# First block of a time-mix and feed-forward kernel: k's first products token tile by token tile, with part of k's weights loaded ahead of x's third tile

## Chip, cores and metric

One core of one Trainium2 chip runs the whole kernel. The metric is the device time of one execution in microseconds (us), read as the median of several runs. Three runs of the kernel before took 940.05, 940.10 and 938.86 us.

## What is computed

For x of shape (4, 1024, 512), float32, with xn the layer norm of x over its last axis, the kernel computes x + attention(xn) + ffn(xn):

```python
xx = concatenate([xn[:, 1:2], xn[:, :-1]], axis=1) - xn      # the token before, less this one
k = (xn + xx * time_mix_k) @ Wk.T                            # 512 -> 704
r = (xn + xx * time_mix_r) @ Wr.T
state_t = state_{t-1} * exp(-exp(time_decay)) + relu(k_t)    # a scan over the tokens
attention = layernorm((state * r) @ Wv.T) * gamma + beta     # 704 -> 512
ffn = (gelu(f16(xn) @ W0.T + bias0)).f16 @ W1.T + bias1      # 512 -> 2048 -> 512
```

Token 0 of a sequence takes token 1 as "the token before".

## The kernel before, in words

The 4096 tokens are cut into eight blocks of 512 tokens (`TB`), each of four tiles of 128 tokens (`NS`). The 512 channels are four chunks of 128 (`NC`), the 704 hidden rows five chunks of 128 and a half chunk. A block is turned so that channels lie on the partitions; then come the products of k and r (`product`, L213), the scan, the output product (L448, L458), and the feed-forward part (`up` L517, `down` L532). Every block but the first is normed and turned while TensorE works on the block before. The first block has nothing ahead of it, so it has a function of its own, `first_inputs`, and only that stretch and its loads are touched by the change.

Loads. All DMAs are issued on SyncE's queue, in the order of the code: x's four tiles (L83, 256 KB each), the two mixing vectors (L108, L109, 2 KB each, as `mix_rows`), k's four weight tiles (L113, 352 KB each), three small loads into `late_rows` (L114 to L116: decay and bias0), r's weights (L118), then W0 and the rest. The issuing engine waits for the DMA eight places earlier to land.

`first_inputs`. Within `tc.manual_schedule` the order on ScalarE, VectorE and TensorE is the order of the code:

- `busy(10)` (L238): ten products of the identity with itself, whose result nobody reads. `mix_rows` is turned on TensorE (L299), and ScalarE copies it out as `mix_sb` and `rest_sb` = 1 - mix (L309, L310).
- Tiles 0 and 1 of x: mean and variance (L186, L187), root on ScalarE (L244), reciprocal on VectorE (L247), normalised (L190), turned on TensorE into the four PSUM tiles `pt` (L254), and `busy(2)`.
- `mixed(0, c, ...)` for half a block (256 tokens) and each chunk c: ScalarE writes rest * now into `xk` (L267), VectorE adds mix * the token before (L279). The first column takes a product on ScalarE (L274, `other`) and a sum on GpSimd (L277).
- `products(c, half)`: for each chunk c three products (hidden chunks 0 to 2) of 128x128 weights with 256 tokens, into the PSUM tiles `pk_0`, `pk_1`, `pk_2`.
- Tiles 2 and 3 are normed and turned while the first half's products run. Between the third and fourth chunk of those products TensorE also turns `late_rows` (L325) into the PSUM tile `tail`. Then the second half is mixed and multiplied.
- ScalarE copies `tail` out as `late_sb` (L332). Then `mixed(1, c, 0, TB)`: the same for r over all 512 tokens, ScalarE into `ar` (pool tag `xx`, two buffers), VectorE into `xnT` (L267, L279).
- After the schedule: ScalarE casts `pt` to float16 (L341), copies the last column (L343), loads another table and makes exp(-exp(decay)) in place (L345, L346).

What follows on TensorE is `full_chunks`: `pr_0`, `pr_1`, `pr_2` (r's products, four of 512 tokens each, from `xnT`), then `pk_3`, `pr_3`, `pk_4`, `pr_4`. On ScalarE `states` reads `pk_0` as `rk_0` (Relu, L389), then `rk_1`, `rk_2`; VectorE scans them (L391).

PSUM. The pool `ps_mm` has four buffers, handed out in turn: `idle`, `small`, `tail`, `pk_0`, then again `pk_1` (idle's), `pk_2` (small's), `pr_0` (tail's), `pr_1` (pk_0's, free once `rk_0` has read it), `pr_2` (pk_1's, after `rk_1`). This order is the same in both kernels.

Of the kernel before, what the change touches and what calls it, by code (L numbers as in the profile page):

```python
# [9 lines left out]
F32 = mybir.dt.float32  # L10
F32R = mybir.dt.float32r
AF = mybir.ActivationFunctionType
ALU = mybir.AluOpType

P = 128
# [4 lines left out]
def time_mix_and_gelu_ffn(  # L20
# [26 lines left out]
    nc = tc.nc  # L47
    B, T, C = x.shape
    HID = wkT.shape[1]
    N = w0T.shape[1]  # L50
    TB = 512
    NS = TB // P
    NC = C // P
    NN = N // P
# [3 lines left out]
    NF = HID // P  # L58
# [5 lines left out]
    def pool(name, bufs, **kw):  # L64
        return ctx.enter_context(tc.tile_pool(name=name, bufs=bufs, **kw))
# [4 lines left out]
    const = pool("const", 1)  # L70
    one = pool("one", 1)
    two = pool("two", 2)
    three = pool("three", 3)
    four = pool("four", 4)
    ps_mm = pool("ps_mm", 4, space=bass.MemoryType.PSUM)
    ps_e = pool("ps_e", 4, space=bass.MemoryType.PSUM)
    dram = pool("dram", 1, space=bass.MemoryType.DRAM)

    def load_x(i):
        b, t0 = blocks[i]  # L80
        xs = one.tile([P, NS, C], F32, tag="x", name=f"x_{i}")
        for s in range(NS):
            nc.sync.dma_start(xs[:, s, :], x[b, t0 + s * P : t0 + (s + 1) * P, :])  # L83
        return xs


    x_now = load_x(0)
    ident = const.tile([P, P], F32, name="ident")
    make_identity(nc, ident)
    nhalf = const.tile([P, NS], F32, name="nhalf")  # L90
# [3 lines left out]
    eps_sb = const.tile([P, 1], F32, name="eps_sb")  # L94
    nc.vector.memset(eps_sb, EPS)
    mix_rows = const.tile([2 * NC, P], F32, name="mix_rows")
    late_rows = const.tile([NF + 1 + NN, P], F32, name="late_rows")
    nc.vector.memset(late_rows, 0.0)
    mix_sb = const.tile([P, 2 * NC], F32, name="mix_sb")
# [5 lines left out]
    def rows(ap):  # L105
        return ap.rearrange("(c p) -> c p", p=P)

    nc.sync.dma_start(mix_rows[:NC], rows(mix_k))  # L108
    nc.sync.dma_start(mix_rows[NC:], rows(mix_r))  # L109
    wk_sb = [const.tile([P, HID], F32, name=f"wk_{c}") for c in range(NC)]  # L110
    wr_sb = [const.tile([P, HID], F32, name=f"wr_{c}") for c in range(NC)]
    for c in range(NC):
        nc.sync.dma_start(wk_sb[c], wkT[c * P : (c + 1) * P, :])  # L113
    nc.sync.dma_start(late_rows[:NF], rows(decay[:H0]))  # L114
    nc.sync.dma_start(late_rows[NF : NF + 1, :HF], decay[H0:].rearrange("(c p) -> c p", p=HF))
    nc.sync.dma_start(late_rows[NF + 1 :], rows(bias0))  # L116
# [59 lines left out]
    def rstd_of(var, name):  # L176

        n = var.shape[1]
        r = two.tile([P, n], F32, tag=f"rstd{n}", name=name)
        nc.gpsimd.tensor_scalar_add(r, var, EPS)  # L180
        nc.gpsimd.tensor_tensor(r, r, nhalf[:, :n], ALU.pow)
        return r

    def stats_of(mv, s, src, name):
        st6 = two.tile([P, 6], F32, tag="st6", name=name)
        nc.vector.bn_stats(st6, src)  # L186
        nc.vector.bn_aggr(mv[:, s, :], st6)  # L187

    def normalize(dst, src, mean, rstd):
        nc.vector.tensor_scalar(dst, src, mean, rstd, ALU.subtract, ALU.mult)  # L190
# [21 lines left out]
    def product(dst, w, cols, src, c):  # L212
        return nc.tensor.matmul(  # L213
            dst, w[c][:, cols], src, start=(c == 0), stop=(c == NC - 1)
        )

    def first_inputs(xs, behind):

        pts = [ps_e.tile([P, TB], F32, tag="pe", name=f"pt_0_{c}") for c in range(NC)]
        idle = ps_mm.tile([P, TB], F32, tag="mm", name="idle")
        small = ps_mm.tile([P, TB], F32, tag="mm", name="small")
        mix_t = small[:, : 2 * NC]
        tail = ps_mm.tile([P, TB], F32, tag="mm", name="tail")
        late_t = tail[:, : NF + 1 + NN]
        mv = two.tile([P, NS, 2], F32, tag="mv", name="mvx_0")
        rstd = two.tile([P, NS], F32, tag=f"rstd{NS}", name="rx_0")  # L230
        xk = one.tile([P, NC, TB], F32, tag="xk", name="xk_0")
        TH = TB // 2
        halves = slice(0, TH), slice(TH, TB)

        def busy(n):

            for _ in range(n):
                nc.tensor.matmul(idle[:, :P], ident, ident, start=True, stop=True)  # L238

        def stats(s):  # L240
            stats_of(mv, s, xs[:, s, :], f"stx_0_{s}")

        def deviations(a, b):
            nc.scalar.activation(rstd[:, a:b], mv[:, a:b, 1], AF.Sqrt, bias=eps_sb)  # L244

        def inverses(a, b):
            nc.vector.reciprocal(rstd[:, a:b], rstd[:, a:b])  # L247

        def normalized(s):
            normalize(xs[:, s, :], xs[:, s, :], mv[:, s, 0:1], rstd[:, s : s + 1])  # L250

        def turned(s):
            for c in range(NC):
                nc.tensor.transpose(  # L254
                    pts[c][:, s * P : (s + 1) * P], xs[:, s, c * P : (c + 1) * P], ident
                )

        def mixed(kind, c, a, b):

            src = pts[c]  # L260
            if kind == 0:
                dst = part = xk[:, c, :]
            else:
                part = two.tile([P, TB], F32, tag="xx", name=f"ar_0_{c}")
                dst = xnT[:, c, 1:]
            j = kind * NC + c
            scaled = nc.scalar.activation(  # L267
                part[:, a:b], src[:, a:b], AF.Identity, scale=rest_sb[:, j : j + 1]
            )

            if a == 0:

                other = four.tile([P, 1], F32, tag="other", name=f"other_{kind}_{c}")
                nc.scalar.activation(  # L274
                    other, src[:, 1:2], AF.Identity, scale=mix_sb[:, j : j + 1]
                )
                nc.gpsimd.tensor_add(dst[:, 0:1], part[:, 0:1], other)  # L277
                a = 1
            added = nc.vector.scalar_tensor_tensor(  # L279
                dst[:, a:b],  # L280
                src[:, a - 1 : b - 1],
                mix_sb[:, j : j + 1],
                part[:, a:b],
                ALU.mult,
                ALU.add,
            )
            return scaled, added

        def products(c, part):
            for h, pk in enumerate(pks):  # L290
                product(pk[:, part], wk_sb, slice(h * P, (h + 1) * P), xk[:, c, part], c)

        with tc.manual_schedule(
            engines={nc.scalar.engine, nc.vector.engine, nc.tensor.engine}
        ):

            nc.scalar.activation(rstd[:, :1], eps_sb, AF.Sqrt)
            busy(10)
            nc.tensor.transpose(mix_t, mix_rows, ident[: 2 * NC, : 2 * NC])  # L299
            stats(0)  # L300
            deviations(0, 1)
            stats(1)
            deviations(1, 2)
            for s in range(NS // 2):
                inverses(s, s + 1)
                normalized(s)
                turned(s)
            busy(2)
            nc.scalar.copy(mix_sb, mix_t)  # L309
            nc.scalar.activation(rest_sb, mix_t, AF.Identity, bias=1.0, scale=-1.0)  # L310
            pks = [ps_mm.tile([P, TB], F32, tag="mm", name=f"pk_0_{h}") for h in range(3)]
            stats(2)
            for c in range(NC):
                if c == NC - 1:
                    stats(3)
                mixed(0, c, 0, TH)
            deviations(2, NS)
            inverses(2, NS)
            normalized(2)
            normalized(3)  # L320
            for c in range(NC):
                if c == NC - 1:
                    turned(2)
                    turned(3)
                    nc.tensor.transpose(  # L325
                        late_t, late_rows, ident[: NF + 1 + NN, : NF + 1 + NN]
                    )
                products(c, halves[0])
            for c in range(NC):
                mixed(0, c, TH, TB)  # L330
                products(c, halves[1])
            nc.scalar.copy(late_sb, late_t)  # L332
            for c in range(NC):
                scaled, added = mixed(1, c, 0, TB)

        behind.enter_context(tc.issue_after(scaled.ins))
        behind.enter_context(tc.issue_after(added.ins))
        x16s = []
        for c, pt in enumerate(pts):
            x16 = four.tile([P, TB], F16, tag="x16", name=f"x16_0_{c}")  # L340
            nc.scalar.copy(x16, pt)  # L341
            x16s.append(x16)
            nc.scalar.copy(last[:, c, :], pt[:, TB - 1 :])  # L343

        nc.scalar.activation(w_sb, w_sb, AF.Exp)  # L345
        nc.scalar.activation(w_sb, w_sb, AF.Exp, scale=-1.0)  # L346
        return x16s, xk, pks
# [214 lines left out]
    state = {}  # L562
    behind = ExitStack()
    x16s, xk, pks = first_inputs(x_now, behind)
    xf = ffn_input(0, x16s)

# [6 lines left out]
    for i in range(len(blocks)):  # L573
# [6 lines left out]
        if more:  # L580

            with tc.issue_after(state["kept"].ins) if i == 1 else nullcontext():
                x_now = load_x(i + 1)
# [76 lines left out]
```

## Time and profile before

| | |
|---|---|
| median of the three runs | 940.05 us |
| the profiled execution, its own time | 939.56 us |
| its span, first instruction to last | 937.5 us |
| TensorE busy | 930.5 us, 99% |
| ScalarE busy | 164.4 us, 18% |
| VectorE busy | 489.0 us, 52% |
| first product of `pk` starts | 8.66 us |
| first product of `pr` starts | 20.33 us |
| granted TensorE clock | 1.00 throughout |

The span lies within the execution's own time; 2.06 us lie around it. Starts are counted from the span's first instruction. A float32 product of 128x128 weights shows as two records of TensorE (MATMUL) with two weight loads (PEld, which overlap it); a turn shows as one. [...] records overlap: what a stream of them costs is the distance from start to start.

### The profile page before, as it was taken

What the parts mean: (1) busy time and instruction counts of PE and PEld (TensorE: products, weight loads), DVE (VectorE), ACT (ScalarE), POOL (GpSimd) and SP (SyncE); (2) the same over time, 40 slices, a digit from 0 to 9 for tenths busy, and PEclk for the clock granted to TensorE, in tenths of its full rate; (3) what the DMA queues carried; (4) which work ended last, traced back from release to release, by engine and by line L of the source; (5) the groups of instructions that cost most, each with busy time, mean ns of one, the idle gap of its engine ahead of it and who ended that gap; (6) DMA issues with size and microseconds to landing.
All of it is one profiled execution on the core that took longest, in us unless ns stands there. A gap on an engine that the chain in (4) does not pass through costs nothing.

```text
span 937.5 us, 8775 instructions
## 1 busy us (share of the span) xinstructions
PE 930.5 (99%) x3266; PEld 591.2 (63%) x3266; DVE 489.0 (52%) x843; ACT 164.4 (18%) x276; POOL 52.5 (6%) x132
## 2 busy tenths in 40 slices
PE   8999999999999999999999999999999999999998
PEld 7448854885448854588545884458844688445686
DVE  6768772733836338353474525755256552642513
ACT  6423410220002200112001220012100121001021
POOL 1010000000100001000010000100011000100100
PEclk9999999999999999999999999999999999999999
DMA  9644660443204432054320543105431044310243
GB/s 318 202 155 157 224 224 0 135 158 113 90 1 157 143 106 90 1 170 143 104 77 0 180 145 114 56 0 195 142 113 45 19 138 152 96 45 1 69 155 113
DMA packets 39718, 106.50 MB, mean 114 GB/s; under 512 B 4447, under 2 KB 4732, under 8 KB 39676
## 3 DMA queue, kind: packets, MB, share of 16 engines
q1 hardware_dynamic: 39676, 105.94, 34.3%
q8 instruction: 26, 0.43, 0.2%
q14 instruction: 16, 0.13, 0.0%
HBM read 89.14 MB, written 16.78 MB: 113 GB/s over the span
## 4 chain that ended last, share of the span: by engine, by line
PE 99%; DMA 0%; SPq 0%; DVE 0%; issue 0%; ACT 0%; DVEq 0%; POOL 0%; ACTq 0%
PE pd L517 25%; PE pe L532 25%; PE po L448 15%; PE pk L213 15%; PE pr L213 15%; PE pkr L213 3%; PE po L458 2%; DMA mix_rows<-in_L_attn_time_mix_r 0%; SPq L83 0%; PE pt L254 0%; DVE e L495 0%; ACT xk L267 0%; DVE z L504 0%; SPq L108 0%; DVEq L656 0%
## 5 line engine op out<-in xcount | busy, mean ns | idle before, releaser
L532 PE MATMUL pe<-w,d 128*128 128x512 f32 x1024 | 250.4, 389 | 0.0
L532 PEld LDWEIGHTS pe<-w,d 128*128 128x128 f32 x1024 | 192.2, 188 | 40.2 <-DVE d L527 0.3
L517 PE MATMUL pd<-xf,w0h 128*128 128x512 f32 x512 | 202.8, 396 | 0.0
L517 PE MATMUL pd<-xf,w0l 128*128 128x512 f32 x512 | 199.5, 390 | 0.0
L527 DVE CAST d<-d 128x512 fp32r<-128x512 f16 x128 | 54.3, 425 | 187.9 <-ACT d L525 186.6
L525 ACT ACTIVATE d<-pd,late_sb 128x512 f16<-128x512 f32 x128 | 87.9, 687 | 352.9 <-PE pd L517 352.9
L213 PE MATMUL pk<-xk,wk 128*128 128x512 f32 (+1 forms) x344 | 144.0, 563 | 0.6 <-POOL xk L277 0.6
L213 PE MATMUL pr<-xnT,wr 128*128 128x512 f32 x320 | 143.7, 592 | 0.0
L448 PE MATMUL po<-wv_sb,g 128*128 128x512 f32 x320 | 140.8, 595 | 0.0
L213 PEld LDWEIGHTS pk<-xk,wk 128*128 128x128 f32 x344 | 65.2, 190 | 72.2 <-issue 67.9
L517 PEld LDWEIGHTS pd<-xf,w0h 128*128 128x128 f32 x512 | 96.1, 188 | 23.2 <-issue 2.3
L517 PEld LDWEIGHTS pd<-xf,w0l 128*128 128x128 f32 x512 | 96.2, 188 | 21.6 <-issue 1.9
L213 PEld LDWEIGHTS pr<-xnT,wr 128*128 128x128 f32 x320 | 60.6, 189 | 76.4 <-issue 74.9
L448 PEld LDWEIGHTS po<-wv_sb,g 128*128 128x128 f32 x320 | 60.2, 190 | 75.8 <-issue 75.0
L207 DVE STREAM_TRANSPOSE xnT<-x 32x512 f32<-32x512 f32 x112 | 78.7, 702 | 5.0 <-PE pkr L213 2.9
L389 ACT ACTIVATE rk<-pk 128x512 f32<-128x512 f32 x40 | 23.9, 597 | 255.7 <-PE pk L213 253.5
L186 DVE BATCH_NORM_STATS2 sty<-po 128x6 f32<-128x512 f32 x32 | 22.1, 691 | 68.3 <-PE po L458 66.1
L391 DVE TENSOR_TENSOR_SCAN st<-late_sb,carry,rk 128x512 f32<-128x512 f32 (+1 forms) x24 | 30.7, 1279 | 43.9 <-ACT rk L389 43.9
L417 DVE TENSOR_TENSOR g<-st,pr 128x512 f32<-128x512 f32 x40 | 27.4, 684 | 39.1 <-PE pr L213 39.1
L391 DVE TENSOR_TENSOR_SCAN st<-late_sb,rk 128x512 f32<-128x512 f32 (+1 forms) x24 | 29.2, 1218 | 32.7 <-ACT rk L389 31.0
L180 POOL TENSOR_SCALAR ry<-mvy 128x1 f32<-128x1 f32 x32 | 11.4, 357 | 436.6 <-DVE mvy L187 436.6
L495 DVE TENSOR_TENSOR e<-pe,b_sb 128x512 f16<-128x512 f32 x32 | 20.2, 685 | 18.3 <-PE pe L532 18.3
(69 smaller groups left out, 455.6 us busy)
## 6 DMA issues: line engine op xcount, KB each, us to landing
w<-w1d SPq DMA_DIRECT2D x111, 512.0 KB, 3.3
x<-in_L_attn_x SPq DMA_DIRECT2D x32, 256.0 KB, 5.2
xres<-in_L_attn_x SPq DMA_DIRECT2D x32, 256.0 KB, 2.7
w1d<-w SPq DMA_DIRECT2D x16, 512.0 KB, 2.9
out<-z SPq DMA_DIRECT2D x31, 256.0 KB, 2.6
w0raw<-in_L_ffn_W SPq DMA_DIRECT2D x16, 256.0 KB, 3.3
w1raw<-in_L_ffn_W SPq DMA_DIRECT2D x16, 256.0 KB, 3.4
wk<-in_L_attn_Wk SPq DMA_DIRECT2D x4, 352.0 KB, 4.9
```

The source lines that it names most:

```text
L186: nc.vector.bn_stats(st6, src)
L207: nc.vector.transpose(dst[i * Q : (i + 1) * Q, :, :, j, :], src[j * Q : (j + 1) * Q, :, :, i, :],)
L213: return nc.tensor.matmul(dst, w[c][:, cols], src, start=(c == 0), stop=(c == NC - 1))
L389: nc.scalar.activation(rk[:hw], pk, AF.Relu)
L391: nc.vector.tensor_tensor_scan(st[:hw], w_sb[:hw, h : h + 1].to_broadcast([hw, TB]), rk[:hw], 0.0 if t0 == 0 else carry[:hw, h : h + 1], A ...
L417: nc.vector.tensor_mul(g[:, h, :], st, pr)
L448: nc.tensor.matmul(pos[s], g[:, h, s * P : (s + 1) * P], wv_sb[:, h, :], start=(first and h == 0), stop=(not first and h == NF - 1),)
L495: nc.vector.tensor_add(e16, pe, b1_sb)
L517: nc.tensor.matmul(pd, w[c][:, cols], xf[:, c, :], start=(c == 0 and w is w0h), stop=(c == NC - 1 and w is w0l),)
L525: state["gelu"] = nc.scalar.activation(d16, pd, AF.Gelu, bias=b0_sb[:, n : n + 1])
L527: nc.vector.tensor_copy(d, d16)
L532: nc.tensor.matmul(pe[s], d[:, s * P : (s + 1) * P], w1[part], start=(n == 0 and part == 0), stop=(n == NN - 1 and part == 1),)
```

## The change

The two `mix_rows` loads go from SyncE's queue to ScalarE's. k's weights come in two parts: columns 0 to 383 of all four tiles (four DMAs of 192 KB) after x's second tile, the remaining 320 columns (four of 160 KB) after x's fourth. In `first_inputs` each token tile of 128 is normed, turned, mixed and multiplied on its own: `products` takes 128 tokens instead of 256. Tile 0 keeps root and reciprocal; tiles 1 to 3 take theirs from `rstd_of` (two instructions on GpSimd, L180, L181). The first column is made by one ScalarE instruction that reads the column just written as its bias. The ten `busy` products become five, then the turn of `mix_rows`, then five; `busy(2)` becomes `busy(3)` after tile 0. The turn of `late_rows` goes behind all products of `pk`.

```diff
-    def load_x(i):
+    def load_x(i, amid=lambda: None):
         b, t0 = blocks[i]
         xs = one.tile([P, NS, C], F32, tag="x", name=f"x_{i}")
         for s in range(NS):
+            if s == NS // 2:
+                amid()
             nc.sync.dma_start(xs[:, s, :], x[b, t0 + s * P : t0 + (s + 1) * P, :])
...
+    FIRST = 3
+    def load_wk(cols):
+        for c in range(NC):
+            nc.sync.dma_start(wk_sb[c][:, cols], wkT[c * P : (c + 1) * P, cols])
+
+    x_now = load_x(0, lambda: load_wk(slice(0, FIRST * P)))
...
-    nc.sync.dma_start(mix_rows[:NC], rows(mix_k))
-    nc.sync.dma_start(mix_rows[NC:], rows(mix_r))
...
-    for c in range(NC):
-        nc.sync.dma_start(wk_sb[c], wkT[c * P : (c + 1) * P, :])
+    nc.scalar.dma_start(mix_rows[:NC], rows(mix_k))
+    nc.scalar.dma_start(mix_rows[NC:], rows(mix_r))
+    load_wk(slice(FIRST * P, HID))
...
         def stats(s):
             stats_of(mv, s, xs[:, s, :], f"stx_0_{s}")
+            var = mv[:, s, 1:]
+            if s == 0:
+                rstds[s] = dev[:, :1]
+                nc.scalar.activation(rstds[s], var, AF.Sqrt, bias=eps_sb)
+                nc.vector.reciprocal(rstds[s], rstds[s])
+            else:
+                rstds[s] = rstd_of(var, f"rx_0_{s}")
...
             if a == 0:
-                other = four.tile([P, 1], F32, tag="other", name=f"other_{kind}_{c}")
-                nc.scalar.activation(
-                    other, src[:, 1:2], AF.Identity, scale=mix_sb[:, j : j + 1]
-                )
-                nc.gpsimd.tensor_add(dst[:, 0:1], part[:, 0:1], other)
+                scaled = nc.scalar.activation(
+                    dst[:, 0:1], src[:, 1:2], AF.Identity, scale=m, bias=part[:, 0:1]
+                )
                 a = 1
...
-            nc.scalar.activation(rstd[:, :1], eps_sb, AF.Sqrt)
-            busy(10)
+            nc.scalar.activation(dev[:, 1:2], eps_sb, AF.Sqrt)
+            busy(5)
             nc.tensor.transpose(mix_t, mix_rows, ident[: 2 * NC, : 2 * NC])
-            stats(0)
-            deviations(0, 1)
-            stats(1)
-            deviations(1, 2)
-            for s in range(NS // 2):
-                inverses(s, s + 1)
-                normalized(s)
-                turned(s)
-            busy(2)
+            busy(5)
             nc.scalar.copy(mix_sb, mix_t)
             nc.scalar.activation(rest_sb, mix_t, AF.Identity, bias=1.0, scale=-1.0)
-            pks = [ps_mm.tile([P, TB], F32, tag="mm", name=f"pk_0_{h}") for h in range(3)]
-            stats(2)
-            for c in range(NC):
-                if c == NC - 1:
-                    stats(3)
-                mixed(0, c, 0, TH)
-            deviations(2, NS)
-            inverses(2, NS)
-            normalized(2)
-            normalized(3)
-            for c in range(NC):
-                if c == NC - 1:
-                    turned(2)
-                    turned(3)
-                    nc.tensor.transpose(
-                        late_t, late_rows, ident[: NF + 1 + NN, : NF + 1 + NN]
-                    )
-                products(c, halves[0])
-            for c in range(NC):
-                mixed(0, c, TH, TB)
-                products(c, halves[1])
+            stats(0)
+            normalized(0)
+            turned(0)
+            busy(3)
+            stats(1)
+            pks = [
+                ps_mm.tile([P, TB], F32, tag="mm", name=f"pk_0_{h}") for h in range(FIRST)
+            ]
+            for s in range(NS):
+                tokens = slice(s * P, (s + 1) * P)
+                for c in range(NC):
+                    if c == NC // 2 and s + 1 < NS:
+                        normalized(s + 1)
+                    mixed(0, c, tokens.start, tokens.stop)
+                for c in range(NC):
+                    if c == NC - 1 and s + 1 < NS:
+                        turned(s + 1)
+                    products(c, tokens)
+                if s + 2 < NS:
+                    stats(s + 2)
+            nc.tensor.transpose(late_t, late_rows, ident[: NF + 1 + NN, : NF + 1 + NN])
             nc.scalar.copy(late_sb, late_t)
             for c in range(NC):
                 scaled, added = mixed(1, c, 0, TB)
```

More of the change, by code (lines that the diff above doesn't have):

```diff
@@ L82, in load_x @@
         for s in range(NS):
+            if s == NS // 2:
+                amid()
             nc.sync.dma_start(xs[:, s, :], x[b, t0 + s * P : t0 + (s + 1) * P, :])
         return xs
-    x_now = load_x(0)
+    FIRST = 3
+    wk_sb = [const.tile([P, HID], F32, name=f"wk_{c}") for c in range(NC)]
+    wr_sb = [const.tile([P, HID], F32, name=f"wr_{c}") for c in range(NC)]
+    def load_wk(cols):
+        for c in range(NC):
+            nc.sync.dma_start(wk_sb[c][:, cols], wkT[c * P : (c + 1) * P, cols])
+    x_now = load_x(0, lambda: load_wk(slice(0, FIRST * P)))
     ident = const.tile([P, P], F32, name="ident")
@@ L106, in rows @@
         return ap.rearrange("(c p) -> c p", p=P)
-    nc.sync.dma_start(mix_rows[:NC], rows(mix_k))
-    nc.sync.dma_start(mix_rows[NC:], rows(mix_r))
-    wk_sb = [const.tile([P, HID], F32, name=f"wk_{c}") for c in range(NC)]
-    wr_sb = [const.tile([P, HID], F32, name=f"wr_{c}") for c in range(NC)]
-    for c in range(NC):
-        nc.sync.dma_start(wk_sb[c], wkT[c * P : (c + 1) * P, :])
+    nc.scalar.dma_start(mix_rows[:NC], rows(mix_k))
+    nc.scalar.dma_start(mix_rows[NC:], rows(mix_r))
+    load_wk(slice(FIRST * P, HID))
     nc.sync.dma_start(late_rows[:NF], rows(decay[:H0]))
@@ L229, in first_inputs @@
         mv = two.tile([P, NS, 2], F32, tag="mv", name="mvx_0")
-        rstd = two.tile([P, NS], F32, tag=f"rstd{NS}", name="rx_0")
+        dev = two.tile([P, NS], F32, tag=f"rstd{NS}", name="rx_0")
+        rstds = {}
         xk = one.tile([P, NC, TB], F32, tag="xk", name="xk_0")
-        TH = TB // 2
-        halves = slice(0, TH), slice(TH, TB)
         def busy(n):
@@ L241, in stats @@
             stats_of(mv, s, xs[:, s, :], f"stx_0_{s}")
[L243 to L247, printed above, removed]
+            var = mv[:, s, 1:]
[5 more added lines that the diff above has]
+                rstds[s] = rstd_of(var, f"rx_0_{s}")
         def normalized(s):
-            normalize(xs[:, s, :], xs[:, s, :], mv[:, s, 0:1], rstd[:, s : s + 1])
+            normalize(xs[:, s, :], xs[:, s, :], mv[:, s, 0:1], rstds[s])
         def turned(s):
@@ L266, in mixed @@
             j = kind * NC + c
+            m = mix_sb[:, j : j + 1]
             scaled = nc.scalar.activation(
@@ L271, in mixed @@
             if a == 0:
-                other = four.tile([P, 1], F32, tag="other", name=f"other_{kind}_{c}")
-                nc.scalar.activation(
-                    other, src[:, 1:2], AF.Identity, scale=mix_sb[:, j : j + 1]
+                scaled = nc.scalar.activation(
+                    dst[:, 0:1], src[:, 1:2], AF.Identity, scale=m, bias=part[:, 0:1]
                 )
-                nc.gpsimd.tensor_add(dst[:, 0:1], part[:, 0:1], other)
                 a = 1
             added = nc.vector.scalar_tensor_tensor(
[L280 to L285, printed above, removed]
+                dst[:, a:b], src[:, a - 1 : b - 1], m, part[:, a:b], ALU.mult, ALU.add
             )
```

## The prediction

> **What bounds the kernel now.** I read the page first. TensorE is busy for the whole span; no other engine comes near.
>
> ```profile
> PE 930.5 (99%) x3266; PEld 591.2 (63%) x3266; DVE 489.0 (52%) x843; ACT 164.4 (18%) x276; POOL 52.5 (6%) x132
> ```
>
> Then the waits of TensorE over the whole span. There are three, all of them ahead of the first product of `pk` at 8.66 us:
>
> ```profile
> PE idle L238 <- POOL ident masks.py:199: 1.3, 1, 1.3
> PE small L299 <- DMA mix_rows<-in_L_attn_time_mix_r: 0.6, 1, 0.6
> PE pk L213 <- POOL xk L277: 0.6, 1, 0.6
> ```
>
> From 8.66 us on TensorE never waits. So whatever makes a product late from there on is paid in full at the end, and only work taken from it, or an earlier start, is a gain. What TensorE does in the first 31 us, from its timeline (start, length, operation):
>
> ```profile
> 1.34 4.45 PE L238 MATMUL idle<-ident 128*128 128x128 f32 x20 [1.34 <-POOL ident masks.py:199]
> ...
> 7.48 0.61 PE L238 MATMUL idle<-ident 128*128 128x128 f32 x4
> 8.66 4.12 PE L213 MATMUL pk<-xk,wk 128*128 128x256 f32 x18 [0.57 <-POOL xk L277]
> 12.62 1.04 PE L254 MATMUL pt<-ident,x 128*128 128x128 f32 x8
> 13.59 0.24 PE L325 MATMUL tail<-ident,late_rows 22*128 22x22 f32 x1
> 13.75 6.74 PE L213 MATMUL pk<-xk,wk 128*128 128x256 f32 x30
> 20.33 10.47 PE L213 MATMUL pr<-xnT,wr 128*128 128x512 f32 x24
> ```
>
> The reader is to see that `tail` is turned at 13.59, in the middle of `pk`. ScalarE's timeline shows what hangs on that:
>
> ```profile
> 14.81 0.20 ACT L332 COPY late_sb<-tail 128x22 f32<-128x22 f32 x1
> 14.87 0.73 ACT L267 ACTIVATE ar<-pt,rest_sb 128x512 f32<-128x512 f32 x1
> ...
> 18.09 0.59 ACT L341 CAST x<-pt 128x512 f16<-128x512 f32 x1
> ...
> 20.40 1.28 ACT L345 ACT_TABLE_LOAD   x1
> 21.70 0.21 ACT L345 ACTIVATE late_sb<-late_sb 128x6 f32<-128x6 f32 x1
> 21.81 0.58 ACT L389 ACTIVATE rk<-pk 128x512 f32<-128x512 f32 x1
> ```
>
> Behind the copy of `tail` stand r's inputs (`ar`), the casts, the table and `rk_0`, which ends at 22.39. All this runs under the products of `pk` and `pr_0`. `pr_1`, which writes into `pk_0`'s buffer, starts at 20.33 + 8 x 0.43 = 23.77 (8 records of `pr_0`; 24 of them take 10.47 less a last one's tail), so `rk_0` has 1.4 us to spare.
>
> **What the Trainium skill says.** "PSUM — Partial Sum Buffer", Engine vs sequencer instructions: ScalarE's queue is strict FIFO, and TensorE's matmuls run in program order, only weight loads being pulled ahead. The timelines agree: `ar` starts 0.06 us behind the copy of `tail`, never ahead of it. "ScalarE: Activation LUTs", What ACT_TABLE_LOAD costs: 1283 ns for a table, here 1.28 us; each pointer operand (scale or bias from a column) adds about 93 ns. Here a 512-column Gelu with a bias takes 687 ns and the Relu without one 597 ns, so it agrees (90). "TensorE: Matmul & The Clock Gate", The HAM clock gate: the array runs at half rate until busy for about 3.4 us and falls back after an idle window of that length. Here the distance of the idle products goes from 0.21 to 0.11 us about 4 us after the first; no idle time after 8.66 tests the fall.
>
> **The change part by part.**
>
> *Loads.* 1.4 MB of weights and 1 MB of x stay what they are; two issues of 0.38 and 0.26 us leave SyncE's queue, four of 0.43 are added to it, each past `late_rows`, r's weights and W0. That is about 1.1 us later for these at most. r's last tile was issued at 9.3 and lands within 5 us, at 14.3; it is needed from 20 us. W0's splits start at 22.4. Cover enough; I take zero. x's tiles 2 and 3 get 0.8 MB ahead of them, some 2 us at the 400 GB/s of 6 to 10 us: they land by about 8.5 and are wanted at 9.4 and 12. k's first columns have some 1.3 MB before and with them: about 6 us, wanted from 7.4. The mixing vectors, issued at 0.7 on ScalarE ahead of its table load, should land by 3.6 (x's first tile takes 2.7 us); if they take a microsecond more the root of tile 0 waits 0.5 us.
>
> *First product.* Mean and variance of tile 0 still start at 3.40 and end at 4.30. Root 4.41 to 4.70, reciprocal 0.13, normalise 0.55, hand-over 0.04 each: 5.45. TensorE is in `busy` until about 5.7 (5 products at 2 x 0.213 = 2.1 us, the turn of the vectors at 3.5, then 2.1 us that speed up at 5.35). First turn 0.33: 6.03. ScalarE: 0.10 to wake, 128 columns 0.35 (0.47 for 256, 0.73 for 512, so 0.13 per 128), then the column: it reads what was just written, so it waits for the end (0.06), and has two pointers (0.25 for L274, plus 0.09): 6.9. VectorE 0.04 + 0.35; TensorE 0.10: 7.4. That is 1.25 us ahead of 8.66.
>
> *Products.* 24 products of 256 tokens become 48 of 128. The idle products are the same shape: (0.61 - 0.275) / 3 = 0.111 us from record to record, so 48 x 0.222 = 10.66 us, against 24 x 2 x 0.216 = 10.36. Turns: 12 x 0.109 = 1.31 against 8 x 0.109 = 0.87. The turn of `late_rows` (0.15) leaves. After each turn the next tile's first `xk` needs 0.27 (turn), 0.10, 0.35, 0.04, 0.35, 0.10 = 1.21 us, while TensorE has three further turns and three products, 1.1 us: about 0.1 us idle, four times. VectorE's 2.5 us a tile and GpSimd's 0.92 (0.36 + 0.57 in the later rows) fit into TensorE's 3.1. So `pk` ends at 7.4 + 10.66 + 1.31 + 0.45 = 19.8 against 20.33: a gain of 0.5, the start half spent.
>
> *The turn of `late_rows`.* It now ends the stretch, at 19.8 + 0.24 = 20.05. ScalarE has the copy ahead of `ar` in its order, so `ar_0` starts at 20.05 + 0.10 + 0.06 = 20.2 instead of 14.87. The first `xnT`: 0.73 (ScalarE), 0.06 + 0.36 (column), 0.04 + 0.75 (VectorE), 0.10: `pr_0` starts at 22.25 instead of 20.33. This is a wait of 2.1 us on TensorE that did not exist: behind it everything.
>
> *`rk_0`.* In the trace of before, `ar_0` to the first cast takes 3.22 us and the cast to the end of `rk_0` 4.30 (18.09 to 22.39: casts, table, exp). The second is unchanged. The first becomes about 4.15: two times 0.73 + 0.06 + 0.36 - 0.10 overlapped, then two `ar` that wait for VectorE to free a buffer. So `rk_0` ends at 20.2 + 4.15 + 4.30 = 28.65, and `pr_1`, next in TensorE's order with nothing to pass it, starts at 28.75. `pr_0` will have ended at about 26.2, so 2.5 us more stand idle. Against 23.77 that is **+5.0 us**. If the column costs no more than before (0.25), four columns and the tile-0 path give back 0.6, and waits of 0.1 that don't occur 0.4: +4.0 is the lower end.
>
> *Behind.* `rk_1` needs the scan of `rk_0` (1.23) and 0.6: 30.6, while `pr_1` runs to 32.2; `pr_2` does not wait. W0's splits start some 6 us later, TensorE 5. The first of them is needed at 48.14 and was complete at 30.13. The tightest is `g_4`: ready at 50.37 for 51.83, and it loses one microsecond of 1.46 but now stands ahead of a split in VectorE's order. I take zero.
>
> Sum: 939.56 + 5.0 = 944.5 for an execution like the profiled one. That one lies 0.5 below the median, so the forecast is 944.7, between 944.5 and 945.0.
>
> **The rivals.**
>
> *The clock falls back.* Two idle stretches of 2.1 and 2.5 us, with 4 us of products between, are each shorter than the window, but the window runs free. If it falls, `pr_1` runs at half rate for some 3.4 us: +1.7, 946.4. For it: nothing in this trace. Against: the gap of 0.63 at 5.8 did not slow what followed.
>
> *The tile stretch is bound by the small engines.* ScalarE and VectorE hand over per chunk; if each chunk of 0.67 us waited another 0.1, 16 of them cost 1.6: 946.2. Against: both have slack of 0.6 us a tile.
>
> *Only the first wait shows.* If `pr_1` did not have to wait for `rk_0`, the loss is 22.25 - 20.33 = 1.9: 941.7. Against: the buffers go round in turn.
>
> *The gain comes through (not slower).* If the copy of `tail` does not hold `ar`, everything for r runs under `pk` as now, and the earlier end of 0.5 counts: 939.3. It decides at one point: `rk_0` must end by 23.7, so with 8.5 us of work from the copy, that must start by 15.2, and the turn it waits for stands behind 48 products that end near 20. Only if the order were not kept.
>
> **How the numbers follow.** The likeliest case, 943.2 to 945.8, has 0.77; clock or small engines 0.15 together (to 946.8); first wait only 0.04; gain 0.04. The range 943.1 to 946.7 leaves out the last two and some of the tails. The measurement tells about 0.2%, 1.9 us, from no change. Slower by more: 0.92; within: 0.06; faster: 0.02.
>
> **What would show it.** `pk`'s first record near 7.4 and 128-token records 0.111 apart; `pr_0` at 22 us behind a wait that ends in VectorE's `xnT`; `pr_1` at 28 to 29 behind ScalarE's `rk`; two new rows in TensorE's waits, 2.1 and 2.5 us. If the copy of `late_sb` runs before 16 us, or `pr_1` starts before `rk_0` ends, the forecast is wrong.

## Result and profile after

The kernel after takes 944.71 us, median of six runs (944.12 to 944.92); six runs of the kernel before beside it took 939.33 us (938.86 to 940.10). The ratio is 1.0051, 95% interval 1.0040 to 1.0062: slower, by 5.4 us. The profiled execution took 944.66 us with a span of 942.9 us. TensorE is still the busy engine; it has 3.4 us more, though the arithmetic is the same (24 products became 48 of half the length).

```profile
PE 933.9 (99%) x3316; PEld 594.1 (63%) x3316; DVE 489.7 (52%) x849; ACT 166.7 (18%) x282; POOL 54.1 (6%) x130
```

TensorE's waits over the whole span (total, times, longest): two new ones, in front of `pr`. The one for `mix_rows` is gone.

```profile
PE pr L222 <- DVE xnT L286: 2.0, 1, 2.0
PE idle L245 <- POOL ident masks.py:199: 1.3, 1, 1.3
PE pr L222 <- ACT rk L383: 0.9, 1, 0.9
PE pk L222 <- DVE xk L286: 0.3, 1, 0.3
```

TensorE's timeline up to 34 us:

```profile
3.97 2.50 PE L245 MATMUL idle<-ident 128*128 128x128 f32 x10
6.27 0.64 PE L263 MATMUL pt<-ident,x 128*128 128x128 f32 x4
6.75 0.83 PE L245 MATMUL idle<-ident 128*128 128x128 f32 x6
7.88 2.29 PE L222 MATMUL pk<-xk,wk 128*128 128x128 f32 x18 [0.29 <-DVE xk L286]
...
16.90 3.63 PE L222 MATMUL pk<-xk,wk 128*128 128x128 f32 x30
20.45 0.23 PE L325 MATMUL tail<-ident,late_rows 22*128 22x22 f32 x1
22.71 5.40 PE L222 MATMUL pr<-xnT,wr 128*128 128x512 f32 x8 [2.03 <-DVE xnT L286]
29.00 5.42 PE L222 MATMUL pr<-xnT,wr 128*128 128x512 f32 x12 [0.89 <-ACT rk L383]
```

`pk` starts 0.78 us earlier than before and ends at the same time, 20.5. Then come the turn of `late_rows`, 2.03 us of nothing, `pr_0`, and again 0.89 us of nothing: `pr_1` starts at 29.00 instead of 23.77. ScalarE's timeline shows what TensorE waits for:

```profile
20.73 0.18 ACT L326 COPY late_sb<-tail 128x22 f32<-128x22 f32 x1 [2.81 <-PE tail L325]
20.80 0.69 ACT L277 ACTIVATE ar<-pt,rest_sb 128x512 f32<-128x512 f32 x1
21.52 0.35 ACT L282 ACTIVATE xnT<-pt,ar,mix_sb 128x1 f32<-128x1 f32 x1
...
24.66 0.57 ACT L335 CAST x<-pt 128x512 f16<-128x512 f32 x1
...
26.96 1.28 ACT L339 ACT_TABLE_LOAD   x1
28.26 0.21 ACT L339 ACTIVATE late_sb<-late_sb 128x6 f32<-128x6 f32 x1
28.37 0.58 ACT L383 ACTIVATE rk<-pk 128x512 f32<-128x512 f32 x1
```

The reader is to see the bracket of the first line: ScalarE stands idle for 2.81 us until TensorE has turned `tail`, though all it needs for `ar` has long been there. From the copy to the end of `rk_0` it never stops again: 8.2 us in one row.

One thing more is in this trace. The eight records of `pr_0` take 6.29 us from 22.71 to 29.00 less 0.89 of waiting: 5.4 instead of 3.44. The granted clock by stretches (stretch; its length, TensorE's busy time and records; **clock**; the two columns for DMA) says why:

```profile
20.00:23.00 3.00, 0.97 (x7) 1.00 0.99 275
23.00:24.00 1.00, 1.00 (x3) 0.71 0.98 227
24.00:27.00 3.00, 3.00 (x5) 0.53 0.97 341
27.00:29.00 2.00, 1.11 (x3) 1.00 0.99 351
```

TensorE ran at half its clock from 23.42 to 26.83 us. Whether that is part of the price was the first open question.

### The profile page after: what moved, and what is told of

Same layout as the page of the kernel before. It is cut to its first block, busy times and chain, and to the rows that moved or that the text cites. A ratio compares the mean times of both kernels' runs of the same rounds, so it can differ in the third digit from the quotient of the medians.

```text
span 942.9 us, 8892 instructions
## 1 busy us (share of the span) xinstructions
PE 933.9 (99%) x3316; PEld 594.1 (63%) x3316; DVE 489.7 (52%) x849; ACT 166.7 (18%) x282; POOL 54.1 (6%) x130
## 4 chain that ended last, share of the span: by engine, by line
PE 98%; ACT 1%; DVE 0%; issue 0%; POOL 0%; DVEq 0%; POOLq 0%; ACTq 0%
PE pd L511 25%; PE pe L526 25%; PE po L442 15%; PE pk L222 15%; PE pr L222 14%; PE pkr L222 3%; PE po L452 2%; PE idle L245 1%; ACT ar L277 0%; ACT x L335 0%; PE pt L263 0%; ACT xnT L282 0%; ACT L339 0%; DVE e L489 0%; ACT rk L383 0%
## 5 line engine op out<-in xcount | busy, mean ns | idle before, releaser
L222 PE MATMUL pr<-xnT,wr 128*128 128x512 f32 x320 | 145.8, 598 | 2.9 <-DVE xnT L286 2.0
L222 PEld LDWEIGHTS pk<-xk,wk 128*128 128x128 f32 x392 | 67.5, 190 | 71.0 <-issue 68.2
```

The lines of the kernel that those rows point to most:

```text
L222: return nc.tensor.matmul(dst, w[c][:, cols], src, start=(c == 0), stop=(c == NC - 1))
```

## Experiments

The theory: ScalarE executes in order, so the late turn of `late_rows` makes everything behind its copy late, first `ar` and `xnT` (the first wait), then, behind the casts and the table, `rk_0` (the second). Rivals: the cutting into tiles of 128 tokens with its small instructions; the loads; the clock.

All kernels in one table (us). "pk", "pr_0", "pr_1" are the first records in the profiled execution; "rest" is that execution's own time less the start of `pr_1`; the runs of before stand beside the median.

| kernel | pk | pr_0 | pr_1 | profiled | rest | median | before beside | ratio, 95% interval |
|---|---|---|---|---|---|---|---|---|
| before | 8.66 | 20.33 | 23.77 | 939.56 | 915.79 | 939.33 | | |
| after | 7.88 | 22.71 | 29.00 | 944.66 | 915.66 | 944.71 | 939.33 | 1.0051 (1.0040–1.0062) |
| e1 turn early | 7.52 | 20.25 | 25.72 | 943.04 | 917.32 | 942.44 | 939.78 | 1.0029 (1.0017–1.0040) |
| e2 before, turn last | 8.96 | 22.44 | 28.24 | 944.06 | 915.82 | 945.25 | 939.78 | 1.0055 (1.0042–1.0068) |
| e3 before, loads | 10.11 | 23.47 | 26.91 | 942.46 | 915.55 | 940.30 | 939.78 | 1.0008 (1.0000–1.0017) |
| e4 Relu first | 7.64 | 22.47 | 27.71 | 943.30 | 915.59 | 943.26 | 939.78 | 1.0036 (1.0023–1.0049) |
| e5 gap busy | 7.31 | 22.29 | 28.46 | 945.89 | 917.43 | 944.92 | 939.80 | 1.0059 (1.0046–1.0072) |
| e6 Relu first, gap busy | 7.32 | 22.29 | 25.92 | 941.52 | 915.60 | 941.60 | 939.80 | 1.0019 (1.0011–1.0028) |
| e7 turn early, Relu first | 9.00 | 22.41 | 25.85 | 941.38 | 915.53 | 939.70 | 939.80 | 1.0001 (0.9992–1.0009) |
| e8 as e7, fewer idle | 7.40 | 20.06 | 23.50 | 939.14 | 915.64 | 938.91 | 939.80 | 0.9991 (0.9983–0.9999) |
| e9 gap partly busy | 7.99 | 22.87 | 26.57 | 942.12 | 915.55 | 941.65 | 939.89 | 1.0022 (1.0013–1.0030) |
| e10 before, mixing vectors | 8.77 | 20.44 | 23.88 | 939.57 | 915.69 | 939.25 | 939.89 | 0.9989 (0.9981–0.9998) |

Read the column "rest" first. But for e1 and e5 (their clock falls behind `pr_1`) it lies within 0.3 us. So nothing behind `pr_1` tells these kernels apart, and each profiled time follows from the start of its `pr_1`.

**e1: only the turn, forward again.**

```diff
                         turned(s + 1)
+                        if s + 2 == NS:
+                            nc.tensor.transpose(late_t, late_rows, ...)
...
-            nc.tensor.transpose(late_t, late_rows, ...)
```

> The kernel after, with only the turn of late_rows moved forward: behind the turn of tile 3, ahead of the last products of tile 2. The cutting into tiles of 128 tokens and the loads stay. If the place of the turn is the cause, ScalarE copies tail right behind its last xk, at about 17.9 us, so everything on ScalarE comes 2.9 us earlier: ar_0 at 17.9 instead of 20.8, rk_0 ends at 26.1 instead of 29.0. pr_0 then follows pk at about 20.5 without a wait, and the one wait left is that of pr_1 for rk_0, about 2.1 us: pr_1 at 26.1, and the time is 941.8 us. If the cutting into tiles, the small engines or the loads are the cause, the place of the turn changes nothing: 944.7.

`ar_0` starts at 17.48 and `rk_0` ends at 25.67; the first wait is gone and the second is as expected:

```profile
PE pr L222 <- ACT rk L386: 1.9, 1, 1.9
```

The six executions split by their mean clock over the span: with 1.000 they took 940.96, 941.79 and 941.83 us, as the theory has it; with 0.998 they took 943.04, 943.58 and 943.58. The profiled one is of the second kind. Its clock by stretches shows the fall right behind the wait that ends at 25.72:

```profile
24.00:27.00 3.00, 1.28 (x2) 0.85 1.01 309
27.00:29.00 2.00, 2.00 (x4) 0.50 1.04 386
29.00:34.00 5.00, 5.00 (x13) 0.95 0.67 213
```

The place of the turn costs 2.3 us by the medians, 2.9 where the clock holds. The rival that the cutting or the loads cost it all falls. My 941.8 left out that the remaining wait brings a fall of the clock half the time.

The wait that is left comes from the rest of the change, as the traces show; no run takes it alone. `ar` needs all four tiles, and tile 3 is turned at 16.11 here, while before both later tiles are turned from 12.62 on. So `ar_0` starts at 17.48 instead of 14.87 although the turn of `late_rows` holds nothing up. The new first-column instruction makes the way from `ar_0` to the first cast 3.90 us instead of 3.22. Together `rk_0` ends 3.28 us later than before, where it had 1.4 to spare: 1.87 us of waiting.

**e2: only the late turn, in the kernel before.**

```diff
-                    nc.tensor.transpose(late_t, late_rows, ...)
                 products(c, halves[0])
...
+            nc.tensor.transpose(late_t, late_rows, ...)
```

> The kernel before, with only the turn of late_rows moved behind all products of pk; first block, loads and halves as before. If the place of the turn is the cause, the loss appears without anything else of the change: pk ends at 20.3, the turn at 20.5, ar_0 at 20.6, pr_0 at 22.4 behind a wait of 1.9 us (the column here takes one ScalarE and one GpSimd instruction that lie beside the column's long sum), pr_1 at 20.6 + 3.2 + 4.3 = 28.2 instead of 23.8: +4.4, 943.7 us. If the cutting, the small engines or the loads are the cause, it stays at 939.3.

```profile
PE pr L213 <- POOL xnT L277: 1.8, 1, 1.8
...
PE pr L213 <- ACT rk L387: 0.4, 1, 0.4
```

The same two waits, and `pr_1` at 28.24 for 28.2 expected: the move of one turn, alone, brings 4.5 of the 5.2 us in the start of `pr_1`, and a median as high as that of the kernel after (945.25 against 939.78). The late turn and the rest of the change each make `rk_0` late, and the later one counts, so the gains and losses of e1 and e2 do not add. In the profiled execution (944.06) the clock fell in `pr_0` and the fall lies ahead of the second wait. Three of the five executions took 945.25 to 945.78; of these there is no trace, so what the 1.2 to 1.7 us above the profiled one are stays open. All five have a mean clock of 0.998; a fall that comes behind the second wait, as in the trace of e5 below, would fit, but is not shown.

**e3 and e10: only the loads, in the kernel before.** e3 takes both parts (as in the change's own diff), e10 only the mixing vectors:

```diff
-    nc.sync.dma_start(mix_rows[:NC], rows(mix_k))
-    nc.sync.dma_start(mix_rows[NC:], rows(mix_r))
+    nc.scalar.dma_start(mix_rows[:NC], rows(mix_k))
+    nc.scalar.dma_start(mix_rows[NC:], rows(mix_r))
```

> The kernel before, with only the change's loads: the mixing vectors on ScalarE's queue, k's weights in two parts around x's third and fourth tile. The prediction took them at nothing: the first product of pk stays at 8.7, pr_1 at 23.8, the time at 939.3 within 0.4. The wait for mix_rows of 0.6 us may go, but the first product waits for xk, not for it. If x's third and fourth tile come too late behind the weights, the second half's products wait, and the time is over 940.3; if the loads bring something that the turn hides in the kernel after, it is under 938.5.

> The kernel before, with only the two mixing vectors on ScalarE's queue; k's weights stay whole and behind all of x. e3 had both parts of the loads, and in its trace the first product of pk came at 10.1 us, because x's third tile landed at 8.7, behind k's weights, and VectorE's mean of that tile stands ahead of the sums of xk in its order. If the weights ahead of x's third tile are the cause, that mean is again at about 6.3 here, the first product at 8.7 or a little earlier, and the time 939.8 within 0.3. If the mixing vectors on ScalarE's queue are the cause, it is as e3: 940.3 and more.

e3 is no benefit, and its trace shows what the old order makes of such loads. VectorE in the kernel before, then in e3 (start, length, operation, and in brackets the idle time ahead of it):

```profile
6.30 0.69 DVE L186 BATCH_NORM_STATS2 stx<-x 128x6 f32<-128x512 f32 x1
...
8.08 1.52 DVE L279 SCALAR_TENSOR_TENSOR xk<-pt,mix_sb,xk 128x255 f32<-128x255 f32 x3 [0.87 <-ACT other L274]
```

```profile
8.70 0.70 DVE L195 BATCH_NORM_STATS2 stx<-x 128x6 f32<-128x512 f32 x1 [2.22 <-DMA x<-in_L_attn_x]
...
9.53 1.26 DVE L288 SCALAR_TENSOR_TENSOR xk<-pt,mix_sb,xk 128x255 f32<-128x255 f32 x3
```

The mean of x's third tile starts 2.4 us later, behind a wait for its DMA, which now follows k's columns; it stands ahead of the sums for `xk` in VectorE's order, so these start at 9.53 instead of 8.08 although tiles 0 and 1 are ready. TensorE idles 1.95 us, and its clock falls: the profiled execution loses 1.45 and another 1.69 (its first product to `pr_1` takes 16.80 instead of 15.11). Three of thirteen executions of e3 took 942.2 to 942.5 like this one, the others 939.9 to 940.8. In e10 that mean starts at 6.59, the first product at 8.77, and the time is 939.25 beside 939.89: the weights ahead of the third tile are what hurt, not the mixing vectors. (That e10 is 0.6 us faster than before is not explained by its trace, where `pr_1` starts at 23.88 for 23.77.) In the kernel after, the mean of tile 2 stands behind tile 0's sums, and no wait for a load shows.

**e4: the turn still last, but `rk_0` ahead of the casts.** `states` is then handed this `rk_0`.

```diff
+            rk0 = two.tile([P, TB], F32, tag="rk", name="rk_0_0", bufs=1)
+            nc.scalar.activation(rk0, pks[0], AF.Relu)
+            nc.scalar.activation(w_sb, w_sb, AF.Exp)
+            nc.scalar.activation(w_sb, w_sb, AF.Exp, scale=-1.0)
             for c in range(NC):
...
-        nc.scalar.activation(w_sb, w_sb, AF.Exp)
-        nc.scalar.activation(w_sb, w_sb, AF.Exp, scale=-1.0)
```

> The kernel after, with the turn still last, but on ScalarE rk_0 (Relu of pk_0) is put ahead of the four casts and the load of the table, directly behind r's inputs. The first wait, that of pr_0, stays at 2.0 us. rk_0 then ends at about 25.3 instead of 29.0. If the second wait is the price of ScalarE's order, it goes, and what is left is how fast pr_0 runs: in the trace of the kernel after, its records are 0.85 us apart from 23.4 on, instead of 0.43. If the slow stretch comes from the idle 2.0 us ahead, it is still there, pr_0 ends at about 28.0 and pr_1 starts there: 943.7 us, only 1.0 less than the kernel after. If the clock stays up, pr_1 starts at 26.2: 941.9. If the queue is not the cause of the second wait, nothing changes: 944.7.

`rk_0` now ends at 25.01 and the second wait is gone from the list, yet the time is only 1.5 us lower, since `pr_0` itself runs at half clock (23 to 24 us, then 24 to 27):

```profile
PE pr L222 <- DVE xnT L286: 2.0, 1, 2.0
```

```profile
23.00:24.00 1.00, 1.00 (x3) 0.50 0.92 225
24.00:27.00 3.00, 3.00 (x6) 0.61 0.99 341
```

`pr_1` starts at 27.71, near the 28.0 of the half-rate branch of the expectation. All five executions have a mean clock of 0.998.

**e5, e6 and e9: TensorE kept busy in the first wait.** e5 is the kernel after, e6 and e9 are e4, with idle products (seven, seven, two) into `tail`, whose result nobody reads.

```diff
             nc.scalar.copy(late_sb, late_t)
+            for _ in range(7):
+                nc.tensor.matmul(tail[:, :P], ident, ident, start=True, stop=True)
```

> The kernel after, with seven idle products of the identity (their result goes into tail, already copied out, and is read by nobody) behind the copy of late_sb, so that TensorE is busy in the 2.0 us ahead of pr_0. If the half-rate stretch of pr_0 comes from that idle time, its records now stay 0.43 us apart, pr_0 ends at about 26.2 instead of 28.1, and the wait for rk_0 grows from 0.9 to 2.4 us: pr_1 still starts at 29.0 and the time is again 944.7, which shows that in the kernel after the fall of the clock is hidden behind rk_0. The longer wait may now bring a fall of its own in pr_1: up to 1.7 more, 946.4. If the fall is part of the price, the time is 943.0.

> e4 (rk_0 ahead of the casts) and the seven idle products of e5 in the wait ahead of pr_0. Neither wait for rk_0 nor idle time is left; what is left of the loss is the first wait alone. If the clock fell for the idle 2.0 us, pr_0 now runs with 0.43 us from record to record, pr_1 starts at 22.7 + 3.5 = 26.2 instead of 27.7, and the time is 1.7 us under that of e4: 941.6. If the clock falls for another reason, the same as e4: 943.3.

> e4 with two idle products instead of e6's seven in the wait ahead of pr_0, so that about 1.3 us of it stay idle. It asks how long a wait TensorE stands before the clock falls: 1.8 to 2.0 us did it in the kernel after, e2 and e4, 0.9 and less did not. If 1.3 us do it too, the time is as e4's, 943.3, or between in some executions; if not, as e6's, 941.6.

The same two stretches as shown for e4, in e6:

```profile
23.00:24.00 1.00, 1.00 (x3) 1.00 1.02 227
24.00:27.00 3.00, 3.00 (x8) 1.00 1.05 356
```

The clock holds, and e6 takes 941.60, 1.7 us less than e4: the idle 2.03 us were the cause of the half rate, and 1.7 us its price. In e5 the same products save nothing:

```profile
PE pr L222 <- ACT rk L385: 2.3, 1, 2.3
```

The time `pr_0` saves becomes waiting for `rk_0`. Executions of e5 whose mean clock was 1.000 took 944.78 to 944.92, as the kernel after; two with 0.998 took 945.89 and 946.38; in the trace of the first of these the clock falls in `pr_1`, behind the 2.28 us of waiting, with nothing to hide it:

```profile
28.00:34.00 6.00, 5.54 (x9) 0.72 0.43 146
```

So in the kernel after the fall costs nothing. Its own runs agree: those with a mean clock of 1.000 took 944.76 and 944.92, the others 944.12 to 944.79. e9, with 0.27 and 1.09 us of idle time left, is as e6 (941.65): waits of that length did not make the clock fall.

**e7 and e8: both waits removed.** e7 is the edits of e1 and e4 together; e8 has besides

```diff
-            busy(5)
+            busy(3)
             nc.scalar.copy(mix_sb, mix_t)
```

in TensorE's order between the turn of `mix_rows` and that of tile 0.

> The kernel after with the turn of late_rows early (as e1) and rk_0 ahead of the casts (as e4). Both waits should be gone: pr_0 at 20.3 right behind pk, rk_0 ends at about 22.1, pr_1 at 23.8. The rest of the change stays: tiles of 128, loads in two parts. By the prediction's sum the earlier start is spent on the shorter products: 939.3, as before, within 0.4. If the cutting costs something else by itself, it is slower than 939.8; if an earlier start comes through, under 938.8.

> e7 with three idle products instead of five ahead of the turn of tile 0. In the kernel after, tile 0 was normed at 5.60 and its turn waited until 6.27 for idle products at half rate. Now it can start at 5.65, and the first product of pk at 7.2 to 7.4 instead of 7.9: 938.8, half a us under e7 and under the kernel before, if the products behind run at full rate from there. If three products less delay the full rate, the first records of pk are 0.22 us apart instead of 0.11 and the half us is given back: 939.3 or more.

e7 is at 939.70 beside 939.80: with the two waits gone, the rest of the change is neither gain nor loss. Cutting and loads are together here; in the kernel after they were not taken apart. (The profiled execution, 941.38, is above all twelve others, 939.48 to 939.78: x's first tile was first read at 4.30 instead of 3.58 and `mix_rows` kept TensorE waiting 0.55 us, so its first product came at 9.00; and the full rate was granted only at 10.66, so the way from there to `pr_0` took 13.41 us for 12.73 in e1.) In e8 the first product comes at 7.40, and TensorE's list of waits is down to the first identity:

```profile
PE idle L245 <- POOL ident masks.py:199: 1.3, 1, 1.3
```

938.91 beside 939.80, ratio 0.9991 (0.9983 to 0.9999): faster than both kernels, by 0.9 us over the kernel before. That is what the change could have brought with the turn in another place, `rk_0` ahead of the casts and two idle products fewer. The gain is small: the interval barely leaves out no change.

## Why the prediction was right

The forecast for an execution like the profiled one was 944.5, and it took 944.66; the median 944.7, and it is 944.71. The sum has three terms, in the start of `pr_1`:

| us against before | predicted | measured |
|---|---|---|
| first product of `pk` | -1.26 (7.4) | -0.78 (7.88) |
| from there to `pr_0` | +3.18 (14.85 for 11.67) | +3.16 (14.83) |
| from `pr_0` to `pr_1` | +3.06 (6.50 for 3.44) | +2.85 (6.29) |
| `pr_1` | +4.98 | +5.23 |

The mechanism held: both waits are there, behind the instructions that were named. That the totals agree to 0.2 us is partly luck. The errors +0.48, -0.02 and -0.21 cancel in part, and what stands behind `pr_1` took 0.13 less. The forecast median also leaned on three runs of before with a median of 940.05; six of them have 939.33, so by medians the loss is 5.4 us for the 4.65 that 944.7 meant.

- *The first product* was 0.5 us late, the largest error of the sum. x's first tile came 0.18 us later, and I let the idle products speed up at 5.35, while here they ran at half rate up to the first turn at 6.27, though tile 0 was normed at 5.60. The code ahead of it is the same in e5 and e6, where it came at 7.31 and 7.32: the full rate does not start at the same time in each execution (6.35 us here, 5.03 in e5, 5.17 in e6; ahead of that the clock column has no figure of its own and reads 1.00, and the distance of the idle products, 0.21, tells the rate). The Trainium skill says so ("TensorE: Matmul & The Clock Gate", What's actually happening: the window is free-running, so the ramp varies from run to run), and I had taken one point for it.
- *The products.* Records 0.112 us apart, as worked out; `pk` takes 12.57 us to the turn for 12.4. (Three turns and three products are 0.99 us by the prediction's own figures, not 1.1. In place of the waits of 0.1 us the trace shows one distance of 0.21 per tile.) The shorter products and the four more turns of x that now stand between them cost 1.06 of the 3.16 us (e1, with the same cutting and no first wait, takes 12.73 from first product to `pr_0`), the first wait 2.10.
- *The first wait*: 2.03 us for 2.1. ScalarE is the engine, the copy of `tail` the place. e1 shows that moving the turn removes it, e2 that it needs nothing else of the change.
- *`rk_0`*: from `ar_0` to the first cast 3.86 us for 4.15, from there to the end of `rk_0` 4.29 for 4.30; it ended at 28.95 for 28.65, late by the first product and by `pk`, and early by the 0.29: two `ar` were to wait for VectorE to free a buffer, and none does (they start 0.97 us apart). That `pr_1` follows at once, 29.00, was right.
- *The second wait* was to be 2.5 us and is 0.89. The start of `pr_1` was right and the start of the waiting wrong: `pr_0` did not end at 26.2, since the clock had fallen. I had this as a rival, in the wrong place (in `pr_1`, +1.7), and what I held against it, that the gap of 0.63 us slowed nothing, says nothing of one of 2 us. A single wait of 1.8 to 2.3 us did it in six kernels. The price was right (1.7, e4 against e6), but in the kernel after, it lies wholly under ScalarE's 8.2 us, which e5 shows.
- *Only the first wait shows* was priced at 941.7; e6, which has just that, takes 941.60. *The gain comes through* was priced at 939.3 with the copy of `tail` by 15.2 us; e7 gets 939.70 with the copy at 19.59 in its trace, as there `rk_0` no longer stands behind the casts.
- *Loads at zero* holds for the kernel after. That it is not a property of the loads is shown by e3: with another order on VectorE they cost 0.5 us in the median and 3.1 in the profiled execution.
- *Behind `pr_1`*, zero: the column "rest".

## What to carry to other kernels

An instruction that costs 0.15 us where it stands can cost 5 us: before moving one, list who reads its result, and everything that stands behind that reader on its engine, down to whoever frees the buffers of the engine that sets the end. Put what the bounding engine waits for first on an in-order engine (here `rk_0`, 0.6 us of work behind 3.7 us of casts and table), and what nothing waits for last. Where the bounding engine must wait for some 2 us, look at its clock behind the wait, and ask of each slow stretch whether another wait hides it: the one removed alone may then bring nothing, as e5 shows.

## What the runs showed of the hardware

A wait of 1.84 to 2.28 us was enough for TensorE's clock to fall to one half: 2.03 us in the kernel after and e4, 1.84 in e2, 1.87 in e1, 1.95 in e3, 2.28 in e5. Waits of 1.09 (e9), 0.89 and 0.6 us were not followed by one; none between 1.1 and 1.8 was tried. The page cited above advises, under Why this matters for your kernels, no idle gaps over about 3 us; here the measurement decides, and 1.84 us was already enough. The fall lasted as long each time: the mean clock over the ten us from 20 to 30 was 0.83 in the kernel after, in e2 and in e4, and over 23 to 33 in e1, so 1.7 us were lost, 3.4 us at half rate. That length agrees with the page's window. The kernel after, then e9:

```profile
20.00:30.00 10.00, 7.08 (x17) 0.83 0.92 292
```

```profile
20.00:30.00 10.00, 8.64 (x27) 1.00 0.96 303
```

When the fall comes can be read from the times at which the clock changes in the traces (us):

| trace | full rate granted | wait | clock falls | from grant to fall |
|---|---|---|---|---|
| after | 6.35 | 20.69 to 22.71 | 23.42 | 17.07 = 5 x 3.413 |
| e1 | 5.60 | 23.85 to 25.72 | 26.08 | 20.48 = 6 x 3.413 |
| e2 | 6.31 | 20.60 to 22.44 | 23.37 | 17.07 = 5 x 3.413 |
| e3 | 7.19 | 8.16 to 10.11 | 10.60 | 3.41 = 1 x 3.413 |
| e4 | 5.84 | 20.45 to 22.47 | 22.90 | 17.07 = 5 x 3.413 |
| e5 | 5.03 | 26.18 to 28.46 | 28.92 | 23.89 = 7 x 3.413 |

The fall comes a whole number of stretches of 3.413 us after the full rate was granted, some 0.4 to 0.9 us behind the end of the wait, and in all six traces the wait lies wholly inside the last of these stretches.

It does not come every time: three of six executions of e1 and two of five of e5 have a mean clock of 0.998, the others 1.000. That a wait which straddles two of these stretches does not make the clock fall would fit this, but no trace here has such a wait.
